# Two feature halves of a tile as one attention task, written to two ring banks and the two auxiliary banks

## The chip, the cores and the metric

The kernel runs on one core of a Trainium2 chip. The metric is the time of one execution on the device in microseconds; the figure for a kernel is the median of several executions. All arithmetic is in fp32.

In the profile, PE is TensorE (matrix products), PEld its loading of weights, ACT ScalarE, DVE VectorE, POOL GpSimd and SP the engine that starts most transfers. A "pass" is one matmul record of the profile: an fp32 matmul of the program with 256 columns is two passes, an fp32 transposition one.

## The reference

A graph attention block on x (128 graphs, 64 nodes, 512 features), with a 64 x 64 adjacency shared by all. The input is normalised first, the two attention layers follow, then a feed-forward part, a second normalisation and the residual:

```
h = relu(layernorm(x))
# layer 1, four heads
Wh = einsum('bnf,hfo->bhno', h, W_heads)            # 512 x 512 for each head
e  = leaky_relu(f1[..., :, None] + f2[..., None, :])  # f1, f2: Wh times the halves of a_heads
attn = softmax(where(adj > 0, e, -1e9))             # 64 x 64 for each graph and head
h = elu(einsum('bhnm,bhmo->bhno', attn, Wh))        # heads laid side by side: 2048 features
# layer 2: the same with W_out (2048 x 512) and one head
out = elu(gat(h, adj, W_out, a_out))
y = relu(out @ w1 + b1) @ w2 + b2 + out
result = x + layernorm(y) * gamma + beta
```

## The kernel before

128 rows of x, which are two graphs, are one tile; there are 64 tiles, and four of them are a group, so there are 16 groups. Two things matter for what follows.

First, layer 1 applies attention to the normalised input before it multiplies by the weights, since attn (h W) = (attn h) W. This "first attention" of a tile is a product of `HN[t]` (128 rows: two graphs of 64 nodes; 512 features) with the attention weights `AT[t]`. Each graph has only its own 64 rows, so a matmul here uses 64 of the 128 rows of TensorE's array, and the two graphs of a tile stand on rows 0 to 63 and 64 to 127. Their results go to two banks of PSUM.

Second, the large products (the four heads `g_a`, the second layer `g_b`, the feed-forward `g_c` and `g_d`) each multiply 2 x 2 blocks by a scheme of seven block products with sums before and after. The attention results `z` are therefore kept as blocks: "11" and "12" for the two feature halves of the first two tiles of a group, "22" for the second half of the last two, and "S1" for the sum of both halves of those (made beforehand in `HNS`).

PSUM is divided into a ring of six banks and two auxiliary banks:

```python
ps = ctx.enter_context(tc.tile_pool(name="ps", bufs=6, space=bass.MemoryType.PSUM))

def bank(name):
    return ps.tile([P, 2, T], FP, tag="mm", name=name)

def aux(shape, name):
    return ps.tile(shape, FP, tag="aux", name=name, bufs=2)
```

The ring holds the sums of the large products and the results of the first attention. The auxiliary banks take transpositions and small products. The transposition of the second layer's output, one for each tile of the group before, is one of them:

```python
def transpose_out(j):
    ...
    pt = aux([P, KC, P], f"pto{g}_{j}")
    for k in range(KC):
        nc.tensor.transpose(pt[:, k, :], o[:, j, ts(k, P)], ident)
    nc.scalar.copy(OT[j // 2][:, :, ts(j % 2, P)], pt)
    nc.gpsimd.tensor_tensor(o[:, j], o[:, j], b2s, ALU.add)
    if j == G - 1:
        bl[1] = blocks(OT, f"o{g}")       # sums of OT, on VectorE
```

The first attention has a task for each tile and feature half, eight in a group. A task takes two ring banks, makes four matmuls (two column blocks `c` for each of two graphs `b`), and ScalarE empties the first bank and VectorE the second:

```python
def task(j, half):
    t = G * g + j
    nm = ("11", "12")[half] if j < 2 else ("S1", "22")[half]
    ...
    src, off = (HNS[t], 0) if nm == "S1" else (HN[t], half * T)
    at = AT[t]
    banks = [bank(f"pz{nm}_{t}_{b}") for b in range(NB)]
    for c in range(2):
        for b in range(NB):
            rows = slice(b * N, (b + 1) * N)
            nc.tensor.matmul(
                banks[b][:, c, :].rearrange("p (h n) -> p h n", h=H),
                src[rows, off + c * P:off + (c + 1) * P],
                at[rows, b], start=True, stop=True, skip_group_check=True,
            )
    for b in range(NB):
        ...
        if b == 0:
            nc.scalar.copy(dst, srcv)
        else:
            nc.vector.tensor_copy(dst, srcv)
```

The statistics of the next tile's x and its normalisation run between these tasks: VectorE makes the statistics (`n1st`) of an x that a transfer must have brought, ScalarE writes `hn`, and this frees the buffer for the next x.

The main loop goes through the groups. While the products of layer 2 of group g run step by step (`project2(g)`, 28 steps of four matmuls each, named `g_b`), side work is laid between the steps: the first attention of group g + 1, the transpositions, feed-forward and output of group g - 1, and the scores of group g + 2:

```python
attn = attend1(g + 1) if g + 1 < NG else []
norms, scores, turns = stage_a(g + 2)
tr, ff, fin = feed_forward(g - 1) if g >= 1 else ([], [], [])
...
first = mix(attn, tr)
if g >= 1:
    first[5:5] = norms[:1]
    first[10:10] = norms[1:]
...
run(project2(g), first + mix(ff[:7] + early + ..., scores + [nothing] * 8) + ...)
```

`mix` merges lists evenly, and `run` spreads the side list evenly over the steps. The first group's attention has no loop to stand in and comes before it. A scheduler then sets each engine's order from priorities and dependences, so the order of the calls is not exactly that of the engine.

Of the kernel before, what the change touches and what calls it, by code (L numbers as in the profile page):

```python
# [9 lines left out]
FP = mybir.dt.float32  # L10
# [12 lines left out]
def gat_preln_kernel(  # L23
# [28 lines left out]
    nc = tc.nc  # L52
    P = 128
    B, N, F = x.shape
    H = W_heads.shape[0]
# [3 lines left out]
    NB = P // N  # L59
    KC = F // P  # L60
    NT = B * N // P
    G = 4
    NG = NT // G
    Q = O // 2
    T = 2 * P
# [6 lines left out]
    big = ctx.enter_context(tc.tile_pool(name="big", bufs=1))  # L72
# [5 lines left out]
# [5 lines that stand above are left out]
# [7 lines left out]
    X, HN, HNS, AT = {}, {}, {}, {}  # L90
# [156 lines left out]
    def flush_late():  # L247
        while late:
            late.pop(0)()

    def run(steps, side=()):

        side, done = list(side), 0
        for i, fn in enumerate(steps):
            fn()
            while done * len(steps) < (i + 1) * len(side):
                side[done]()
                done += 1
# [204 lines left out]
    def transpose_weights(p):  # L463
        A = A1.pop(p)
        for j in range(2):
            t = 2 * p + j


            pt = aux([P, NB * H, N], f"s1pt{t}")
            for h in range(H):  # L470
                to = pt[:, h:h + H + 2:H + 1] if h + 1 < H else pt[:, h:h + 2]
                nc.tensor.transpose(to, A[:, j, h:h + 2].rearrange("p b m -> p (b m)"), ident)  # L472
            AT[t] = big.tile([P, NB, H, N], FP, tag="at", name=f"at{t}", bufs=G)
            nc.scalar.copy(AT[t].rearrange("p b h n -> p (b h) n"), pt)  # L474
# [5 lines left out]
    def stage_a(g):  # L480


        if g >= NG:
            return [], [], []
        p, r = 2 * g, 2 * g + 1

        def norms(p):
            norm1(2 * p)
            norm1(2 * p + 1)
            if p >= 2:  # L490
                prefetch(2 * p + 2)
                prefetch(2 * p + 3)

        def transposes(p):
            transpose_h(2 * p)
            transpose_h(2 * p + 1)

        return (
            [lambda: norms(p), lambda: norms(r)],
            [  # L500
                lambda: transposes(p), lambda: transposes(r), nothing, lambda: project_f(g), nothing,
                lambda: (scores1(g), attn_weights(p)), nothing, lambda: attn_weights(r),
            ],
            [nothing, lambda: transpose_weights(p), nothing, nothing, lambda: transpose_weights(r)],
        )
# [4 lines left out]
    def attend1(g):  # L510
        z = {}
        ZB[g] = z

        def task(j, half):
            t = G * g + j
            nm = ("11", "12")[half] if j < 2 else ("S1", "22")[half]
            if nm not in z:
                z[nm] = big.tile([P, H, 2, T], FP, tag="z" + nm, name=f"z{nm}_{g}")
            src, off = (HNS[t], 0) if nm == "S1" else (HN[t], half * T)
            at = AT[t]  # L520
            banks = [bank(f"pz{nm}_{t}_{b}") for b in range(NB)]
            for c in range(2):
                for b in range(NB):
                    rows = slice(b * N, (b + 1) * N)
                    nc.tensor.matmul(  # L525
                        banks[b][:, c, :].rearrange("p (h n) -> p h n", h=H),
                        src[rows, off + c * P:off + (c + 1) * P],
                        at[rows, b], start=True, stop=True, skip_group_check=True,
                    )
            for b in range(NB):  # L530
                n0 = (j % 2) * P + b * N
                dst = z[nm][:, :, :, n0:n0 + N].rearrange("p h c n -> p c h n")
                srcv = banks[b].rearrange("p c (h n) -> p c h n", h=H)
                if b == 0:
                    nc.scalar.copy(dst, srcv)
                else:
                    nc.vector.tensor_copy(dst, srcv)

        return [lambda j=j, half=half: task(j, half) for j in range(G) for half in range(2)]


    H1, ZSUM = {}, {}
# [14 lines left out]
    def z_sums(g, h):  # L557
        z = ZB[g]
        ZSUM[h] = new_sums(f"z{g}_{h}")
        eng = nc.vector if (g, h) == (0, 0) else nc.gpsimd  # L560
        sums(eng, z["S1"][:, h], z["11"][:, h], z["12"][:, h], z["22"][:, h], *ZSUM[h])
# [71 lines left out]
    def scores2(g, j):  # L633
        if j == 0:
            F2[g] = sm.tile([P, 2, G], FP, tag="f2", name=f"f2_{g}")
        f = F2[g]
        for c in range(2):
            junk = wk.tile([P, FO], FP, tag="elu", name=f"jf{g}_{j}_{c}", bufs=3)
            nc.vector.scalar_tensor_tensor(  # L639
                junk, WH2[g][:, j], 1.0, ao[:, c, :], ALU.mult, ALU.mult,  # L640
                accum_out=f[:, c, j:j + 1],
            )

    def spread2(g):

        f = F2[g]
        dg = sm.tile([P, G, N], FP, tag="s2dg", name=f"s2dg{g}", bufs=1)
        nc.vector.tensor_tensor(
            dg, eye[:, None, :].to_broadcast([P, G, N]), f[:, 1][:, :, None].to_broadcast([P, G, N]),
            ALU.mult,  # L650
        )
        F2[g] = f, dg
# [26 lines left out]
    def stage_e(g):  # L679

        gap = [lambda: None]
        score = [lambda j=j: scores2(g, j) for j in range(G)]
        attend = [lambda j=j: attend2(g, j) for j in range(G)]
        return (
            gap + score + [lambda: spread2(g)] + gap * 2 + [lambda: softmax2(g)] + gap * 5
            + [lambda: transpose_weights2(g)] + gap * 2 + attend[0:2] + gap + attend[2:4] + gap * 3
        )
# [71 lines left out]
    def mix(*lists):  # L759

        lists = [l for l in lists if l]
        keyed = [((i + 0.5) / len(l), n, fn) for n, l in enumerate(lists) for i, fn in enumerate(l)]
        return [fn for _, _, fn in sorted(keyed, key=lambda k: k[:2])]
# [21 lines left out]
    softmax_end = LAST["A"]  # L785
    transpose_weights(0)
    attn = attend1(0)
    for fn in attn[:4]:
        fn()
    head0 = project1(0, 0)  # L790
    for fn in head0[:2]:
        fn()
    transpose_weights(1)
    for fn in attn[4:]:
        fn()
    z_sums(0, 0)

# [13 lines left out]
    def more_sums(m):  # L811
        fetch(m)
        weight_sums(m, softmax_end)
# [3 lines left out]
    for g in range(NG):  # L817
        if g >= 1:
            side = stage_e(g - 1)
        else:  # L820
            side = sum(stage_a(1), [])
            for i, m in ((5, 4), (9, 5), (12, 6), (17, 7)):
                side.insert(i, lambda m=m: more_sums(m))
        done, n = 0, 6 * H
        for i in range(n):
            if i % 6 == 0:
                steps = head0 if (g, i) == (0, 0) else project1(g, i // 6)
            if (g, i // 2) != (0, 0):
                steps[i % 6]()
            while done * n < (i + 1) * len(side):  # L830
                side[done]()
                done += 1
        flush_late()
# [3 lines that stand above are left out]
        if g == NG - 1:  # L837
            run(project2(g), tr + [nothing] * 6 + ff[:2])
            run(ff[2:], [
                lambda: [scores2(g, j) for j in range(G)], lambda: spread2(g), nothing, nothing,  # L840
                lambda: softmax2(g), *[nothing] * 7, lambda: transpose_weights2(g), nothing,
                *[lambda j=j: attend2(g, j) for j in range(G)], nothing,
            ])
            continue
        early = [lambda: z_sums(g + 1, 0)]
        first = mix(attn, tr)
        if g >= 1:
            first[5:5] = norms[:1]
            first[10:10] = norms[1:]
        if g == 0:  # L850
            def sums_late(m):
                fetch(m)
                weight_sums(m, LAST["A"])

            run(project2(g), first + early + norms + scores + turns + [
                load_rows, lambda: sums_late(M1), lambda: sums_late(M2)
            ])
        else:
            run(project2(g), first + mix(
                ff[:7] + early + ff[7:12] + fin[:1] + ff[12:13] + fin[1:2] + ff[13:],  # L860
                scores + [nothing] * 8,
            ) + mix(fin[2:], [nothing] + turns + [nothing] * 2))
    last = fin
    tr, ff, fin = feed_forward(NG - 1)
# [30 lines left out]
```

## Time and profile before

The kernel takes 2364.29 us, the median of three executions (2364.02 to 2364.8). The profiled execution has a span of 2360.4 us at a mean granted TensorE clock of 0.992.

| What | Value |
|---|---|
| first attention, pz and pzS (line 525), passes | 768 + 256 |
| ScalarE copy of one bank to z (line 535) | 585 ns, 96 for z and 32 for zS |
| VectorE copy of one bank to z (line 537) | 691 ns, 96 for z and 32 for zS |
| large products, one pass (lines 307, 322) | 379 to 385 ns recorded, 1.73 us from start to start for eight |
| transposition pto (line 700), records | 256, for 64 tiles |
| idle of the weight loads before line 525, put down to "issue" | 37.1 us in 119 places |

The times in a row of the profile are the lengths of single records. Records of TensorE overlap, since its passes are pipelined, so eight passes of 380 ns do not take 3 us. What eight passes cost is the distance from the start of the first to the start of what comes after them. "Issue" is idle time for which the profile shows no releaser: nobody was waited for.

### The profile page before, as it was taken

What the parts mean: (1) busy time and instruction counts of PE and PEld (TensorE: products, weight loads), DVE (VectorE), ACT (ScalarE), POOL (GpSimd) and SP (SyncE); (2) the same over time, 40 slices, a digit from 0 to 9 for tenths busy, and PEclk for the clock granted to TensorE, in tenths of its full rate; (3) what the DMA queues carried; (4) which work ended last, traced back from release to release, by engine and by line L of the source; (5) the groups of instructions that cost most, each with busy time, mean ns of one, the idle gap of its engine ahead of it and who ended that gap; (6) DMA issues with size and microseconds to landing.
All of it is one profiled execution on the core that took longest, in us unless ns stands there. A gap on an engine that the chain in (4) does not pass through costs nothing.

```text
span 2360.4 us, 32849 instructions
## 1 busy us (share of the span) xinstructions
PE 2317.9 (98%) x11805; PEld 1934.5 (82%) x11805; DVE 1265.5 (54%) x2210; ACT 911.0 (39%) x1623; POOL 1026.7 (43%) x917
## 2 busy tenths in 40 slices
PE   6989999999999999999999999999999999999997
PEld 4868787888878888787887878888788887878885
DVE  7625474554646556474554745556464563744527
ACT  2524425253352533425244251533525344251513
POOL 5664444416344353443524444253443534533333
PEclk7999999999999999999999999999999999999999
DMA  8545353444535445353444544435354453534443
GB/s 308 184 142 193 125 183 127 164 152 132 182 125 178 134 139 179 126 180 129 154 163 129 182 131 161 153 130 181 127 177 132 138 179 127 182 118 164 157 148 106
DMA packets 257809, 366.89 MB, mean 155 GB/s; under 512 B 22216, under 2 KB 145128, under 8 KB 257648
## 3 DMA queue, kind: packets, MB, share of 16 engines
q1 hardware_dynamic: 251024, 343.82, 43.9%
q0 software_dynamic: 4512, 16.78, 1.9%
q10 hardware_dynamic: 2112, 4.19, 0.5%
q8 instruction: 95, 1.56, 0.3%
q14 instruction: 66, 0.54, 0.1%
HBM read 337.45 MB, written 27.26 MB: 155 GB/s over the span
## 4 chain that ended last, share of the span: by engine, by line
PE 94%; DVE 2%; ACT 1%; POOL 1%; issue 0%; DMA 0%; DVEq 0%
PE g_b L322 33%; PE g_a L307 32%; PE g_c L307 8%; PE g_d L322 8%; PE pz L525 4%; PE pa L673 2%; PE pto L700 1%; PE pzS L525 1%; PE pth L371 1%; PE s1pt L472 1%; PE pf L381 1%; PE s1pe L406 1%; DMA x<-in_x_dram 0%; PE s2pt L667 0%; PE pwa L193 0%
## 5 line engine op out<-in xcount | busy, mean ns | idle before, releaser
L322 PE MATMUL g_b<-w,h 128*128 128x256 f32 x2560 | 598.1, 381 | 0.0
L322 PEld LDWEIGHTS g_b<-w,h 128*128 128x128 f32 x2560 | 480.5, 190 | 72.2 <-issue 10.1
L307 PE MATMUL g_a<-z,w 128*128 128x256 f32 x1520 | 361.0, 380 | 1.2 <-DVE g_a L581 0.7
L307 PE MATMUL g_a<-zs_z,w 128*128 128x256 f32 x1504 | 347.9, 379 | 0.0
L307 PEld LDWEIGHTS g_a<-z,w 128*128 128x128 f32 x1520 | 287.6, 190 | 57.9 <-issue 14.3
L307 PEld LDWEIGHTS g_a<-zs_z,w 128*128 128x128 f32 x1504 | 284.8, 190 | 50.5 <-issue 14.3
L322 PE MATMUL g_b<-w,hS 128*128 128x256 f32 x1024 | 243.5, 382 | 0.0
L585 POOL TENSOR_TENSOR hS<-hS,h 128x512 f32<-128x512 f32 x64 | 83.0, 1297 | 366.8 <-DVE hS L549 366.8
L547 ACT ACTIVATE exc<-g_a 128x512 f32<-128x512 f32 x256 | 152.3, 595 | 199.7 <-DVE g_a L581 119.6
L322 PEld LDWEIGHTS g_b<-w,hS 128*128 128x128 f32 x1024 | 191.4, 191 | 30.9 <-issue 6.7
L549 DVE SCALAR_TENSOR_TENSOR h<-exc,g_a 128x512 f32<-128x512 f32 x192 | 131.6, 686 | 136.3 <-ACT exc L548 136.2
L548 ACT ACTIVATE exc<-exc 128x512 f32<-128x512 f32 x256 | 161.6, 631 | 6.5
L615 POOL TENSOR_TENSOR h<-h,h 128x512 f32<-128x512 f32 x64 | 86.7, 1362 | 138.1 <-PE g_b L322 138.0
L332 POOL TENSOR_TENSOR zs_z<-zS,z 128x512 f32<-128x512 f32 x63 | 89.7, 1424 | 128.3 <-PE g_a L307 123.7
L615 POOL TENSOR_TENSOR h<-hS,h 128x512 f32<-128x512 f32 x64 | 81.1, 1268 | 142.4 <-PE g_b L322 142.4
L474 ACT COPY at<-s1pt 128x512 f32<-128x512 f32 x64 | 34.7, 588 | 279.8 <-PE s1pt L472 279.8
L307 PE MATMUL g_c<-ot,w 128*128 128x256 f32 x512 | 123.9, 385 | 0.8 <-DVE n2ve L347 0.8
L322 PE MATMUL g_d<-w,rt 128*128 128x256 f32 x512 | 121.5, 380 | 1.7 <-DVE o L740 1.0
L307 PE MATMUL g_a<-zS,w 128*128 128x256 f32 x496 | 117.2, 379 | 0.0
L639 DVE SCALAR_TENSOR_TENSOR jf<-wh,ao 128x512 f32<-128x512 f32 x128 | 94.3, 776 | 40.3 <-ACT wh L621 40.1
L333 POOL TENSOR_TENSOR zs_z<-z,zs_z 128x512 f32<-128x512 f32 x63 | 85.4, 1357 | 61.1 <-PE g_a L307 40.7
L307 PEld LDWEIGHTS g_c<-ot,w 128*128 128x128 f32 x512 | 93.9, 190 | 21.8 <-issue 9.3
(159 smaller groups left out, 3535.6 us busy)
## 6 DMA issues: line engine op xcount, KB each, us to landing
w<-tc SPq DMA_DIRECT2D x632, 256.0 KB, 2.6
w<-in_L_gnn_W_heads_dram SPq DMA_DIRECT2D x192, 256.0 KB, 2.7
w<-in_L_gnn_W_out_dram SPq DMA_DIRECT2D x192, 256.0 KB, 2.7
w<-in_L_gnn_w_dram SPq DMA_DIRECT2D x96, 256.0 KB, 2.7
x<-in_x_dram SPq DMA_DIRECT2D x66, 256.0 KB, 3.6
xr<-in_x_dram SPq DMA_DIRECT2D x64, 256.0 KB, 2.8
out_dram<-o SPq DMA_DIRECT2D x64, 256.0 KB, 2.1
tc<-pt POOLq DMA_DIRECT2D x20, 512.0 KB, 5.6
```

Of the source, the lines that this page charges most:

```text
L307: nc.tensor.matmul(bk[:, o, :], w[:, k, ts(o, P)], a[:, k, :], start=start and o == 0 and k == 0, stop=k == 1, skip_group_check=True,)
L322: nc.tensor.matmul(bk[:, j, :], a[:, k, ts(j, P)], w[:, k, :], start=start and k == 0 and j == 0, stop=i == len(ms) - 1 and k == 1, skip_g ...
L332: eng.tensor_tensor(s2, s1, a11, ALU.subtract)
L333: eng.tensor_tensor(s4, a12, s2, ALU.subtract)
L525: nc.tensor.matmul(banks[b][:, c, :].rearrange("p (h n) -> p h n", h=H), src[rows, off + c * P:off + (c + 1) * P], at[rows, b], start=True ...
L547: nc.scalar.activation(ex, src, AF.Relu, scale=-1.0)
L548: nc.scalar.activation(ex, ex, AF.Exp, scale=-1.0)
L549: nc.vector.scalar_tensor_tensor(dst, ex, -1.0, src, ALU.add, ALU.max)
L585: nc.gpsimd.tensor_tensor(dst, dst, H1["22"][:, h], ALU.add)
L615: nc.gpsimd.tensor_tensor(dst[:, h], x0[:, h], x1[:, h], ALU.subtract)
L639: nc.vector.scalar_tensor_tensor(junk, WH2[g][:, j], 1.0, ao[:, c, :], ALU.mult, ALU.mult, accum_out=f[:, c, j:j + 1],)
L673: nc.tensor.matmul(pa, AT2[g][:, j, :], WH2[g][:, j, :], start=True, stop=True)
```

## The change

The two tasks of a tile become one: eight matmuls on 64 rows follow each other, and then come the four copies. The first half is written to two ring banks as before, the second half to the two auxiliary banks, so that a task has four banks at once without taking four of the ring. It is meant to let TensorE do its work on 64 rows in longer runs. The side list has four tasks in place of eight; four empty entries keep its length, so that the other side work stands at the same steps as before. The attention of the first group is split in two blocks of two tiles, as before.

```diff
--- before.py
+++ after.py
@@ -511,32 +511,40 @@
         z = {}
         ZB[g] = z
 
-        def task(j, half):
+        def task(j):
+
             t = G * g + j
-            nm = ("11", "12")[half] if j < 2 else ("S1", "22")[half]
-            if nm not in z:
-                z[nm] = big.tile([P, H, 2, T], FP, tag="z" + nm, name=f"z{nm}_{g}")
-            src, off = (HNS[t], 0) if nm == "S1" else (HN[t], half * T)
             at = AT[t]
-            banks = [bank(f"pz{nm}_{t}_{b}") for b in range(NB)]
-            for c in range(2):
+            done = []
+            for half in range(2):
+                nm = ("11", "12")[half] if j < 2 else ("S1", "22")[half]
+                if nm not in z:
+                    z[nm] = big.tile([P, H, 2, T], FP, tag="z" + nm, name=f"z{nm}_{g}")
+                src, off = (HNS[t], 0) if nm == "S1" else (HN[t], half * T)
+                if half == 0:
+                    banks = [bank(f"pz{nm}_{t}_{b}") for b in range(NB)]
+                else:
+                    banks = [aux([P, 2, T], f"pz{nm}_{t}_{b}") for b in range(NB)]
+                for c in range(2):
+                    for b in range(NB):
+                        rows = slice(b * N, (b + 1) * N)
+                        nc.tensor.matmul(
+                            banks[b][:, c, :].rearrange("p (h n) -> p h n", h=H),
+                            src[rows, off + c * P:off + (c + 1) * P],
+                            at[rows, b], start=True, stop=True, skip_group_check=True,
+                        )
+                done.append((nm, banks))
+            for nm, banks in done:
                 for b in range(NB):
-                    rows = slice(b * N, (b + 1) * N)
-                    nc.tensor.matmul(
-                        banks[b][:, c, :].rearrange("p (h n) -> p h n", h=H),
-                        src[rows, off + c * P:off + (c + 1) * P],
-                        at[rows, b], start=True, stop=True, skip_group_check=True,
-                    )
-            for b in range(NB):
-                n0 = (j % 2) * P + b * N
-                dst = z[nm][:, :, :, n0:n0 + N].rearrange("p h c n -> p c h n")
-                srcv = banks[b].rearrange("p c (h n) -> p c h n", h=H)
-                if b == 0:
-                    nc.scalar.copy(dst, srcv)
-                else:
-                    nc.vector.tensor_copy(dst, srcv)
-
-        return [lambda j=j, half=half: task(j, half) for j in range(G) for half in range(2)]
+                    n0 = (j % 2) * P + b * N
+                    dst = z[nm][:, :, :, n0:n0 + N].rearrange("p h c n -> p c h n")
+                    srcv = banks[b].rearrange("p c (h n) -> p c h n", h=H)
+                    if b == 0:
+                        nc.scalar.copy(dst, srcv)
+                    else:
+                        nc.vector.tensor_copy(dst, srcv)
+
+        return [lambda j=j: task(j) for j in range(G)]
 
 
     H1, ZSUM = {}, {}
@@ -785,13 +793,13 @@
     softmax_end = LAST["A"]
     transpose_weights(0)
     attn = attend1(0)
-    for fn in attn[:4]:
+    for fn in attn[:2]:
         fn()
     head0 = project1(0, 0)
     for fn in head0[:2]:
         fn()
     transpose_weights(1)
-    for fn in attn[4:]:
+    for fn in attn[2:]:
         fn()
     z_sums(0, 0)
 
@@ -843,7 +851,7 @@
             ])
             continue
         early = [lambda: z_sums(g + 1, 0)]
-        first = mix(attn, tr)
+        first = mix(attn, tr, [nothing] * len(attn))
         if g >= 1:
             first[5:5] = norms[:1]
             first[10:10] = norms[1:]
```

## The prediction, made before the changed kernel ran

> **What bounds the kernel now.** I read the busy times first, then the chain of waits, then TensorE's waits, and last one stretch of TensorE's timeline instruction by instruction.
>
> ```profile
> PE 2317.9 (98%) x11805; PEld 1934.5 (82%) x11805; DVE 1265.5 (54%) x2210; ACT 911.0 (39%) x1623; POOL 1026.7 (43%) x917
> ...
> PE 94%; DVE 2%; ACT 1%; POOL 1%; issue 0%; DMA 0%; DVEq 0%
> ```
>
> TensorE is busy 98% of the span and makes up 94% of the chain; no other engine is above 54%. The list of TensorE's waits on others adds up to only some 34 us, and nearly all of it lies before 160 us or after 2300 us. Its longest entries:
>
> ```profile
> PE pzS L525 <- DVE z L537: 5.5, 1, 5.5
> PE s1pt L472 <- DVE s1A L435: 5.4, 1, 5.4
> PE pab L158 <- DMA ar<-in_L_gnn_a_heads_dram: 5.4, 1, 5.4
> ```
>
> So in the middle of the run time can only be won by giving TensorE less to do. The timeline of TensorE in the attention part of one group (start, length, what, number of passes) shows that it does more than its arithmetic there:
>
> ```profile
> 389.85 1.13 PE L525 MATMUL pz<-at,hn 64*128 64x256 f32 x8
> 390.91 1.99 PE L322 MATMUL g_b<-w,h 128*128 128x256 f32 x8
> 392.83 1.13 PE L525 MATMUL pz<-at,hn 64*128 64x256 f32 x8
> 393.90 0.66 PE L700 MATMUL pto<-ident,o 128*128 128x128 f32 x4
> 394.39 1.89 PE L322 MATMUL g_b<-w,h 128*128 128x256 f32 x8
> 396.21 1.13 PE L525 MATMUL pz<-at,hn 64*128 64x256 f32 x8
> 397.28 1.99 PE L322 MATMUL g_b<-w,h 128*128 128x256 f32 x8
> ```
>
> Read the starts. An undisturbed `g_b` step, between two others of full height, takes 1.73 from start to start (median of 167): eight passes of 0.216. A pz task is four matmuls on 64 rows. The two of a pair run on the two halves of the rows at once, so its eight passes are four pairs, which should take 4 x 0.216 = 0.864. It takes 1.06 or 1.07. The `g_b` step after it takes 1.92 where it stands between two pz tasks. One task and the step together: 1.07 + 1.92 = 2.99, where 0.864 + 1.73 = 2.59 would do. **0.40 us go to entering and leaving the 64-row form**, 0.20 each way. Cut finer, the starts in the task at 392.83 fall so: the last `g_b` pass starts at 392.52 and the first pz pair 0.31 later instead of 0.216; the second pair at 393.15 (0.32 later), the third at 393.37 and fourth at 393.58 (0.22, 0.21); the `pto` at 393.90 (0.32). At each change of form both the last interval before it and the first after it are 0.10 long. A short transposition takes 0.49 after a task against 0.44 elsewhere.
>
> **What the Trainium skill says.** "TensorEngine Tiling (Array Packing)", section Key Properties, says that a change of tiling mode, not of the tile, drains the TensorE. The trace agrees and gives the price, 0.20 per change. The same page under PSUM Bottleneck says that tiling makes TensorE faster but not the emptying of PSUM; here a 0.864 us task fills two banks that ScalarE and VectorE empty in 0.585 and 0.691 us, so it holds. "Perfetto Trace Analysis", section Tensor Engine Instruction (MATMUL, LD_WEIGHTS), says that TensorE's recorded ends are an estimate and that ScalarE and VectorE keep strict order. I therefore work with TensorE's starts; the order shows below, where a copy stands behind a waiting statistic.
>
> **The change part by part.**
>
> *Removed: changes of form.* Two tasks of four pairs become one of eight, so a group of four tiles has 4 entries and exits, not 8. Two tasks that already stand next to each other show that nothing is lost between them: in the first group pzS starts at 59.56 and the next pz at 60.52, 0.96 = 0.864 + 0.10, and only the entry's interval is in it. A long task then takes 1.07 + 0.864 = 1.93.
>
> In the built order of the changed kernel the sequence from the first task to the first `g_c` is: pz, g(1)+pto+g(3), pz, g(1)+pto+g(3), g, pz, g(1)+pto+g(3), g, pz, g(1)+pto+g(3), where g is a `g_b` step of four matmuls. That is 4 x 1.93 + 6 x 1.73 + 4 exits x 0.10 + 3 further entries x 0.10 + 4 pto x 0.44 = 7.72 + 10.38 + 0.70 + 1.76 = 20.56. Before, the same work from 388.19 to the `g_c` at 410.02 takes 21.83, and the exit of its last task puts another 0.10 on the `g_c`: 21.93. **Saved: 1.37 per group.** There are 15 loops with first attention; 14 of them look like this one (loop 0 has no pto and waits otherwise, see below). 14 x 1.37 = 19.2 us, all on the path, since TensorE is the path.
>
> *Added: a wait for an auxiliary bank.* The second half of a tile is now written to the two auxiliary banks, which are also those of pto, and pto comes right behind. In the built order each pto is put behind the first `g_b` matmul, and in all 56 cases waits for ScalarE: it takes the bank whose second-half copy ScalarE makes. Count from the task's start. The passes end by the record at 1.13 + 0.864 = 2.00. ScalarE's copy starts 0.04 after that (median over the present tasks) and takes 0.585: ends 2.63. TensorE starts about 0.06 after a release (136.28 to 136.34, and 54.53 to 54.58). So pto can start at 2.69. TensorE is there at 1.93 + 0.10 + 0.43 = 2.46, plus up to 0.10 if the exit costs both its intervals ahead of it; I use 2.55. Gap: 0.14 each, 56 x 0.14 = **7.8 us given back**. This is the term I trust least. The first half's copy is no trouble: it can start at 1.17 and is done at 1.75, before the second one is ready.
>
> *Moved: the order on ScalarE and VectorE.* ScalarE now does both copies, then `hn`, then `ot`. The `ot` of a tile is done some 4.0 after the task's start; the next task's second half, which needs that bank, starts 5.4 after it. VectorE's statistics of the next x wait for a DMA, as now:
>
> ```profile
> 394.00 0.58 ACT L535 COPY z<-pz 128x512 f32<-128x512 f32 x1 [1.63 <-PE pz L525]
> 395.02 0.70 DVE L343 BATCH_NORM_STATS2 n1st<-x 128x6 f32<-128x512 f32 x1 [3.21 <-DMA x<-in_x_dram]
> 395.64 0.68 DVE L537 COPY z<-pz 128x512 f32<-128x512 f32 x1
> ```
>
> Here a copy of z stood ready at about 394.0 and was made at 395.64, because the statistics stood ahead of it for 3.21 us. In the changed order both copies of the second tile stand behind it. By the same durations they are done about 8.8 after the first task's start; the first that needs their bank is the third tile, which starts at 10.7. About 2 us of room. The sums of `ot` on VectorE (1.6 to 1.8 us each beside GpSimd) have 2 to 3 us of room before the second `g_c` product.
>
> *Start.* In the first group the tasks already stand in two blocks, so no change of form is removed, but the later halves must wait for two auxiliary banks instead of the ring: one copy of 0.69 in each block, about +1 us together.
>
> *Loop 0.* TensorE waits 5.5 us at the third tile for VectorE, which stands in the statistics until x arrives at 135.0. In the changed order two copies rather than one stand between that arrival and the bank: 136.28 becomes some 137.5, but TensorE is then half a task further (1.06). I count 0.
>
> Sum: 2364.3 - 19.2 + 7.8 + 1.0 = **2353.9 us**.
>
> **The rivals.**
>
> *A: the wait for the bank takes all of it.* It needs 0.34 at each pto (19.2 / 56) instead of 0.14. For: the release comes within a fraction of a microsecond of the moment it is wanted, and anything on ScalarE ahead of the copy counts in full. Against: ScalarE is busy 39% and has nothing between the two copies. It would make about 2362 to 2364, and above if hn came first.
>
> *B: the wait is hidden and the full gain appears.* For: the exit's intervals may fall ahead of pto as a whole and the release may be a little earlier. Then 2345 to 2347.
>
> *C: VectorE becomes the bound in this stage*, because its copies bunch behind the statistics' DMA and the third tile waits for its auxiliary bank. If that happened in each group by 1 us, 14 us: about 2368. Against: the 2 us of room above, and VectorE's 54%.
>
> *D: the changes of form are hidden anyway.* Against it stands the regularity of the starts, 1.06 and 1.92 in each group, with no wait on anything. I give it little.
>
> **Range and chances.** The centre is the sum. B is the lower end, A the upper: 2345 to 2362. All rivals lie within 1% of the time before. 2% is 47 us, which is nearly all that the changes of form of 128 tasks cost (128 x 0.40 = 51), and the change takes away less than half of them. So within 2% is nearly sure.
>
> **What would show it.** Right: pz in blocks of 16 passes with 1.93 from start to start; the `pto` after a quarter of a `g_b` step; a new line among TensorE's waits, pto on ScalarE's z, of about 8 us over 56 times; the weight loads' idle time at the pz line (531 in the changed kernel) for "issue" about half its present 37 us. Wrong, if that new line is above 15 us or absent (A or B), if pz waits for VectorE in every group (C), or if blocks of 16 passes take 2.1 or more, which would be a cost between the halves that I left out.

## The result, and the profile after

The changed kernel takes **2359.15 us** (median of four executions, 2357.45 to 2361.88). The kernel before, run beside it, takes 2364.23 us (2364.02 to 2364.8). The ratio is 0.9979, with a 95% interval of 0.9962 to 0.9997: 5.1 us less, where 10.4 had been forecast. The sign was right and the size was half.

The share of busy time and the engines' share of the chain, from the profile of the changed kernel:

```profile
PE 2312.2 (98%) x11805; PEld 1938.7 (82%) x11805; DVE 1241.0 (53%) x2210; ACT 911.9 (39%) x1623; POOL 1022.9 (43%) x917
...
PE 92%; POOL 2%; DVE 2%; DMA 1%; ACT 1%; issue 1%; SPq 0%; DVEq 0%; POOLq 0%; ACTq 0%
```

TensorE still shows 98%. That number cannot tell what happened, as will be seen. The Trainium skill, "Perfetto Trace Analysis", section Identifying the Most-Contended Engine, says that the busy share of matmuls is no good measure of how close TensorE is to its limit, because matmuls are pipelined. The runs here agree: 98% is what the profiles of e4 (2340 us) and e5 (2332 us) show as well.

What TensorE waited for on other engines is spread over two lists, that of the matmuls and that of the weight loads ahead of them (what waited, for whom, total in us, times, longest). These are the lines of the matmuls that name a tile of the first attention or a `pto`, in the changed kernel:

```profile
PE pz L531 <- DVE z L545: 6.6, 2, 6.2
...
PE pto L708 <- ACT ot L709: 0.7, 1, 0.7
```

The second list, that of the weight loads, first before and then after:

```profile
PEld pz L525 <- issue: 27.0, 88, 0.3
...
PEld pto L700 <- issue: 18.5, 56, 0.3
...
PEld pzS L525 <- issue: 10.1, 31, 0.3
```

```profile
PEld pto L708 <- ACT z L543: 26.2, 56, 0.5
...
PEld pzS L531 <- issue: 10.1, 31, 0.3
PEld pz L531 <- issue: 9.9, 30, 0.3
```

Two things are to be seen. The gaps at the entries into the 64-row form were 27.0 + 10.1 = 37.1 us in 119 places and are 20.0 in 61: half, because there are half as many entries. And the 56 gaps of `pto` that had no releaser now have one, ScalarE's copy of `z`. The same wait is not in the matmuls' list at all.

The timeline of TensorE in the attention of one group (start, length, what, passes) shows what it costs:

```profile
388.57 2.00 PE L531 MATMUL pz<-at,hn 64*128 64x256 f32 x16
390.50 0.70 PE L322 MATMUL g_b<-w,h 128*128 128x256 f32 x2
391.29 0.66 PE L708 MATMUL pto<-ident,o 128*128 128x128 f32 x4
391.78 1.46 PE L322 MATMUL g_b<-w,h 128*128 128x256 f32 x6
393.17 2.00 PE L531 MATMUL pz<-at,hn 64*128 64x256 f32 x16
```

A block of 16 passes takes 1.93 from start to start. Then come two `g_b` passes, which should take 2 x 0.216 + 0.10 for the exit = 0.53. The `pto` starts 0.79 after them, so it is 0.26 late. In the four places of this group the distance is 0.79, 0.74, 0.80 and 0.74: on average 0.235 late. All 56 places are like this: the `pto` starts 2.72 after its task in 28 of them and 2.67 in the other 28. The `pto` itself takes 0.49 rather than 0.44. Together that is **0.28 to 0.29 at each `pto`**.

The releaser is in the timeline of all engines over the same stretch:

```profile
390.65 0.58 ACT L543 COPY z<-pz 128x512 f32<-128x512 f32 x1 [0.28 <-PE pz L531]
390.71 0.69 DVE L545 COPY z<-pz 128x512 f32<-128x512 f32 x1 [0.17 <-PE pz L531]
391.13 0.82 ACT L359 ACTIVATE hn<-x,n1nb,n1rs 128x512 f32<-128x512 f32 x1
391.29 0.42 PEld L708 LDWEIGHTS pto<-ident,o 128*128 128x128 f32 x4 [0.50 <-ACT z L543]
```

ScalarE's copy of the second half ends at 390.65 + 0.58 = 391.23, and the `pto` starts 0.06 later in the bank that this copy emptied.

By stage, from the starts in the two traces:

| Stretch | before | after |
|---|---|---|
| first pz from the start of the span | 49.05 | 50.21 |
| from there to the third group's pz (the first two groups' attention, with loop 0) | 196.18 | 195.66 |
| one group period, 13 times, each within 0.01 | 142.96 | 142.70 |
| of it, first task to the first `g_c` | 21.83 | 21.68 |
| from the last group's pz to the end | 256.7 | 256.4 |
| span | 2360.4 | 2357.4 |

The period is the measure to trust: it repeats thirteen times to a hundredth. The first pz, which no edit of this study touches, stands anywhere from 49.05 to 50.91 in the eleven traces.

### The profile page after: what moved, and what is told of

Same layout as the page of the kernel before. It is cut to its first block, busy times and chain, and to the rows that moved or that the text cites. A ratio compares the mean times of both kernels' runs of the same rounds, so it can differ in the third digit from the quotient of the medians.

```text
span 2357.4 us, 32812 instructions
## 1 busy us (share of the span) xinstructions
PE 2312.2 (98%) x11805; PEld 1938.7 (82%) x11805; DVE 1241.0 (53%) x2210; ACT 911.9 (39%) x1623; POOL 1022.9 (43%) x917
## 4 chain that ended last, share of the span: by engine, by line
PE 92%; POOL 2%; DVE 2%; DMA 1%; ACT 1%; issue 1%; SPq 0%; DVEq 0%; POOLq 0%; ACTq 0%
PE g_b L322 32%; PE g_a L307 31%; PE g_c L307 8%; PE g_d L322 8%; PE pz L531 4%; PE pa L681 2%; PE pto L708 2%; PE pzS L531 1%; PE s1pt L472 1%; PE pth L371 1%; ACT z L543 1%; PE s1pe L406 1%; DMA pw<-in_L_gnn_W_out_dram 1%; PE pf L381 1%; PE s2pt L675 0%
## 5 line engine op out<-in xcount | busy, mean ns | idle before, releaser
L322 PEld LDWEIGHTS g_b<-w,h 128*128 128x128 f32 x2560 | 479.1, 190 | 71.5 <-issue 10.1
L557 DVE SCALAR_TENSOR_TENSOR hS<-exc,g_a 128x512 f32<-128x512 f32 x64 | 44.0, 687 | 126.5 <-ACT exc L556 125.1
```

The source lines that it names most:

```text
L322: nc.tensor.matmul(bk[:, j, :], a[:, k, ts(j, P)], w[:, k, :], start=start and k == 0 and j == 0, stop=i == len(ms) - 1 and k == 1, skip_g ...
L557: nc.vector.scalar_tensor_tensor(dst, ex, -1.0, src, ALU.add, ALU.max)
```

## The theories

**W, the wait.** The longer blocks save what they should, and sharing the auxiliary banks with `pto` gives nearly all of it back. Then every way of freeing `pto` from that bank makes the kernel some 17 us faster than the changed one.

**B, the block.** Sixteen passes in a row, or the new order of the copies, cost something that the forecast left out. Then freeing `pto` gains little.

**R, the ring.** The auxiliary banks were needed: with all four banks out of the ring of six, the attention and the large products would wait for ring banks instead.

| Run | time, us | ratio to before (95%) | group period |
|---|---|---|---|
| before | 2364.23 | 1 | 142.96 |
| the change | 2359.15 | 0.9979 (0.9962 to 0.9997) | 142.70 |
| e1, `pto` a whole step later | 2342.59 | 0.9904 (0.9889 to 0.9919) | 141.55 |
| e2, `pto` in the ring | 2339.96 | 0.9891 (0.9877 to 0.9906) | 141.37 |
| e3, first half in the auxiliary banks | 2339.59 | 0.9893 (0.9876 to 0.9909) | 141.37 |
| e4, all four banks from the ring | 2340.09 | 0.9892 (0.9877 to 0.9907) | 141.37 |
| e5, two tiles in a block, ring | 2332.41 | 0.9864 (0.9849 to 0.9878) | 140.91 |
| e6, four tiles in a block, ring | 2355.54 | 0.9960 (0.9945 to 0.9975) | 142.5 |
| e7, VectorE frees the bank | 2373.86 | 1.0039 (1.0025 to 1.0053) | 143.91 |
| e8, e4 with the changes of form put back | 2365.45 | 1.0005 (0.9997 to 1.0014) | 143.20 |
| e9, e5 with a quarter in the auxiliary banks | 2335.18 | 0.9871 (0.9855 to 0.9888) | 141.17 |

e1 to e4 take the wait away in four ways, e7 lengthens it, e8 puts back the cost that the change removes, and e5, e6 and e9 ask how far the idea carries. Each ratio is against runs of the kernel before beside it.

## e1: `pto` behind a whole step

The change is left as it is, except for the place of `tr` (the `pto`) in the side list:

```diff
         if g >= 1:
-            first[5:5] = norms[:1]
-            first[10:10] = norms[1:]
+            n0, n1 = norms or [nothing] * 2
+            first = [
+                attn[0], nothing, nothing, tr[0], attn[1], n0, nothing,
+                tr[1], attn[2], nothing, n1, tr[2], attn[3], tr[3],
+            ]
```

> The changed kernel with each pto moved behind a whole g_b step (just ahead of the next task) instead of behind its first matmul; banks unchanged. Theory W (the wait of pto for the auxiliary bank that ScalarE empties costs 0.26 at each of 56 places and another 0.05 for starting again behind it): the wait is gone, a group takes 142.70 - 1.2 = 141.5 us, and the time falls by 14 x 1.2 = 17 us to about 2342. Rival B (the blocks of 16 passes or the changes of form themselves cost what is missing, the wait only stands where they would show anyway): a group stays at 142.7 and the time at 2358 to 2360. Rival O (later transpositions delay the feed-forward's sums): a new wait of g_c for VectorE, and less than half of the 17 us.

Measured: 2342.59 us (2341.66 to 2344.69), a period of 141.55. From the first task to `g_c` it is 20.52. The forecast had 20.56 for this stretch without any wait, so its sum of passes, entries and exits was right. TensorE's timeline shows the same block of 1.93, and no gap at `pto`:

```profile
386.40 2.00 PE L531 MATMUL pz<-at,hn 64*128 64x256 f32 x16
388.33 1.99 PE L322 MATMUL g_b<-w,h 128*128 128x256 f32 x8
390.16 0.60 PE L708 MATMUL pto<-ident,o 128*128 128x128 f32 x4
390.69 2.00 PE L531 MATMUL pz<-at,hn 64*128 64x256 f32 x16
```

The `pto` comes 1.83 after the step's start, which is 8 x 0.216 + 0.10 for the exit; it takes 0.44, and the 0.53 to the next task hold 0.10 for the entry besides. What the changed kernel takes beyond this, 21.68 - 20.52 = 1.16 per group, is the wait with the 0.05 of the slower start behind it. B is refuted here: blocks, copies and the auxiliary banks are those of the changed kernel. The expectation's rival O does not show either: the matmuls' list has 1.4 and 0.8 us of `g_c` waiting for VectorE in the whole run, against 1.3 and 0.8 in the changed kernel.

## e2: `pto` in a ring bank

```diff
-        pt = aux([P, KC, P], f"pto{g}_{j}")
+        pt = bank(f"pto{g}_{j}").rearrange("p a b -> p (a b)").rearrange("p (k q) -> p k q", k=KC)
```

> The changed kernel with pto written to a ring bank instead of an auxiliary one; the scheduler then sets it directly behind the task. Theory W: no wait for the task's own copies, pto costs 0.49 with the exit in it: a group 4 x 1.93 + 4 x 0.49 + 6 x 1.73 + 3 x 0.10 = 20.36 in this stretch instead of 21.67, so 141.4 us per group and about 2341. Rival B: 142.7 per group and 2358 to 2360. Rival R (six ring banks are too few when pto takes one too): a wait of pz or g_b for a copy of 0.3 or more in each group, and a time between the two.

Measured: 2339.96 us (2337.7 to 2341.73), period 141.37. The second halves stay in the auxiliary banks, and only their neighbour has gone. That is 1.33 per group less than the changed kernel, and 0.18 less than e1, where `pto` stands behind a `g_b` step: in e2, as in e3 and e4, it stands directly behind the block (see e4).

## e3: the first half in the auxiliary banks

```diff
-                if half == 0:
+                if half == 1:
                     banks = [bank(f"pz{nm}_{t}_{b}") for b in range(NB)]
```

> The changed kernel with the banks of the halves exchanged: first half in the auxiliary banks, second in the ring. ScalarE's copy of the first half ends some 1.80 after the task's start and TensorE is free for pto at 1.93, so Theory W expects no wait (or under 0.05): a group 141.4 and a time of about 2341. The next task's first half now needs the bank that ot is copied from, at about 4.14 by ScalarE's order, and starts at about 4.15: if that is late it costs up to 0.1 once in a group, 1.4 us in all. Rival B: 142.7 and 2358 to 2360.

Measured: 2339.59 us (2339.07 to 2341.41), period 141.37. `pto` still takes its bank from the attention, but from the half whose copies were done 0.86 earlier. The weight loads' list of e3 still names the copies:

```profile
PEld pto L708 <- ACT zS L543: 9.3, 28, 0.3
PEld pto L708 <- ACT z L543: 9.3, 28, 0.3
```

Together 18.6 us, yet this costs nothing. In e4, where `pto` shares no bank with the attention, the same gap of 0.33 is there without a releaser:

```profile
PEld pto L705 <- issue: 18.5, 56, 0.3
```

It is the exit from the 64-row form. A releaser's name beside a gap thus doesn't make it a loss; only the distance of the starts does.

## e4: all four banks from the ring

The long blocks alone, without the second part of the change:

```diff
-                if half == 0:
-                    banks = [bank(f"pz{nm}_{t}_{b}") for b in range(NB)]
-                else:
-                    banks = [aux([P, 2, T], f"pz{nm}_{t}_{b}") for b in range(NB)]
+                banks = [bank(f"pz{nm}_{t}_{b}") for b in range(NB)]
```

> The changed kernel with all four banks of a task from the ring, none from the auxiliary ones (the merging alone, without the second part of the change). Theory W: pto never waits; the second half of a group's first task waits for VectorE to read the last bank of the head before (about 0.3 once per group), so about 141.7 per group and 2345. Rival R (the ring of six is too small for tasks of four, which is what the auxiliary banks were taken for): waits of pz or g_b for z copies of 1 us or more in a group, and a time at or above 2359.

Measured: 2340.09 us (2338.84 to 2340.89), period 141.37. R is refuted: no wait for a ring bank appears in the groups, not even the 0.3 per group that the expectation had allowed for. TensorE's timeline:

```profile
387.49 2.00 PE L528 MATMUL pz<-at,hn 64*128 64x256 f32 x16
389.42 0.66 PE L705 MATMUL pto<-ident,o 128*128 128x128 f32 x4
389.91 1.89 PE L322 MATMUL g_b<-w,h 128*128 128x256 f32 x8
391.73 2.00 PE L528 MATMUL pz<-at,hn 64*128 64x256 f32 x16
```

Here `pto` follows the block directly, at 1.93, and takes 0.49. A tile's round from task to task is 4.24; in the changed kernel it is 393.17 - 388.57 = 4.60.

From the first task to `g_c` e4 takes 20.34. The work before takes 21.93 with the exit counted (the prediction's figure), so four entries and four exits fewer save 21.93 - 20.34 = 1.59, nearly 4 x 0.40; the periods say the same, 142.96 - 141.37. **The price of a change of form that the prediction read from the trace is what e4 collects.** The auxiliary banks, meant to make the long block possible, cost 142.70 - 141.37 = 1.33 per group: 1.16 for the wait, and the rest because the order built around them puts `pto` behind a `g_b` matmul, as in e1, rather than directly behind the block.

## e5: two tiles in one block

e4, and the blocks twice as long, so that a group has two entries and exits, not four:

```diff
-        return [lambda j=j: task(j) for j in range(G)]
+        return [lambda j=j: (task(j), task(j + 1)) for j in range(0, G, 2)]
...
+            first = [
+                attn[0], tr[0], no, no, tr[1], n0, no,
+                attn[1], tr[2], no, n1, no, tr[3], no,
+            ]
```

> All banks from the ring (as the third alternative above), and the tasks of two tiles as one block of 32 passes, two blocks in a group; the transpositions follow in later steps. If a change into the 64-row form and back costs 0.40 us whatever stands around it, two fewer of them in a group save 0.80: 141.38 - 0.80 = 140.58 per group and 2340.1 - 11 = about 2329. It also needs the two copying engines to keep up with TensorE inside a block (ScalarE 0.585 and VectorE 0.691 for each 0.864 of passes, and ScalarE's normalisation of 0.82 falls between them). Rival: they do not, pz waits for z copies inside the block, and the gain is under half of it.

Measured: 2332.41 us (2330.15 to 2335.29), period 140.91. This is the fastest version, 1.36% below the kernel before (interval 1.22 to 1.51%). The gain over e4 is 0.46 per group where 0.80 was possible. TensorE's timeline:

```profile
391.97 1.13 PE L528 MATMUL pzS<-at,hns 64*128 64x256 f32 x8
392.94 1.03 PE L528 MATMUL pz<-at,hn 64*128 64x256 f32 x8
393.80 1.10 PE L528 MATMUL pzS<-at,hns 64*128 64x256 f32 x8
394.67 1.15 PE L528 MATMUL pz<-at,hn 64*128 64x256 f32 x8
395.75 0.66 PE L705 MATMUL pto<-ident,o 128*128 128x128 f32 x4
```

The block takes 395.75 - 391.97 = 3.78 instead of 0.20 + 4 x 0.864 = 3.66. The quarters start on time (2.70 = 0.10 + 3 x 0.864), but their recorded lengths grow from 1.03 to 1.10 and 1.15: in the third quarter the second of the two passes that should run at once falls 0.07 behind, in the fourth 0.12, and so the last quarter takes 1.08 instead of 0.96. That is 0.24 per group. The lists name no releaser for it; e9 asks for its cause. The remaining 0.10 is that a change of form which ends in a transposition costs less than one that ends in a `g_b` step, see e8.

## e6: four tiles in one block

```diff
+        both = lambda: [fn() for fn in attn]
...
+            first = [
+                both, tr[0], no, no, tr[1], n0, no,
+                no, tr[2], no, n1, no, tr[3], no,
+            ]
```

> As e5_two_tiles, but all four tiles of a group as one block of 64 passes. By the price of changes alone 1.20 below the ring version: 140.2 per group and about 2323. Against it: VectorE's statistics stand between the copies and wait for an x that is only sent for when ScalarE has normalised the tile, so by the durations of the profile a bank is freed some 7.7 us after the block's start and wanted at 5.3; I expect 2 to 3 us of waiting of pz for VectorE in each group, and 2355 to 2370. If the first figure is measured, the copies are no limit.

Measured: 2355.54 us (2353.7 to 2356.55), periods from 140.77 to 144.34, mostly near 142.5. The matmuls' list of waits and TensorE's timeline:

```profile
PE pzS L528 <- DVE z L542: 28.9, 13, 11.4
```

```profile
397.07 1.14 PE L528 MATMUL pzS<-at,hns 64*128 64x256 f32 x8 [1.41 <-DVE z L542]
398.04 1.04 PE L528 MATMUL pz<-at,hn 64*128 64x256 f32 x8
399.01 0.66 PE L705 MATMUL pto<-ident,o 128*128 128x128 f32 x4
```

This block began at 389.76 and takes 9.25, where 0.20 + 8 x 0.864 = 7.11 would do: 2.1 are lost, as the expectation had it. By themselves the copies would keep up, since they empty two banks in about 0.7 and TensorE fills two in 0.864. But ScalarE has a normalisation for each tile besides (2 x 0.585 + 0.82 = 1.99, against 1.73 of TensorE), and VectorE has the statistics of the next x ahead of one of its copies and waits with them for the transfer, as its timeline shows:

```profile
395.73 0.69 DVE L343 BATCH_NORM_STATS2 n1st<-x 128x6 f32<-128x512 f32 x1 [2.26 <-DMA x<-in_x_dram]
396.35 0.67 DVE L542 COPY z<-pz 128x512 f32<-128x512 f32 x1
```

The copy ends at 397.02, and TensorE goes on at 397.07. In the blocks of the last two groups VectorE has no statistics to make, and they take 7.56 (still with ScalarE's normalisations) and 7.23 (without), where the twelve blocks before them take 9.07 to 10.47. So most of the loss is this wait, and not the length of the block. In the short blocks the same order of VectorE has room to wait; a block of sixteen banks has none. Of the 28.9 us, 11.4 fall in loop 0, where x comes late, and 17.5 in twelve later groups.

## e7: VectorE frees the bank

The copies change places: VectorE takes the bank that ScalarE had, and the other way round.

```diff
-                    if b == 0:
+                    if b == 1:
                         nc.scalar.copy(dst, srcv)
```

> The changed kernel with the copies of the two banks exchanged between ScalarE and VectorE, so that pto waits for VectorE (0.691 a copy instead of 0.585, started 0.06 later, and held up behind the statistics in the second tile). TensorE's work is the same. Theory W: pto 0.17 later in each of four places and some 0.5 in the second: a group 143.4 to 143.8 and a time of 2368 to 2374, slower than before the change. Rival B (the wait is only apparent): 142.7 and 2359.

Measured: 2373.86 us (2373.41 to 2374.31), period 143.91 in most groups (two of thirteen have 144.3 and 143.2): **the wait is now longer, and the changed kernel becomes slower than the one before.** The releaser in both lists follows the edit, and with the longer wait it appears in the matmuls' list too, half of the times:

```profile
PE pto L708 <- DVE z L545: 15.4, 28, 1.3
```

```profile
PEld pto L708 <- DVE z L545: 41.9, 56, 1.7
```

TensorE's timeline has a short and a long one:

```profile
390.19 0.70 PE L322 MATMUL g_b<-w,h 128*128 128x256 f32 x2
391.11 0.66 PE L708 MATMUL pto<-ident,o 128*128 128x128 f32 x4 [0.22 <-DVE z L545]
...
394.92 0.70 PE L322 MATMUL g_b<-w,h 128*128 128x256 f32 x2
396.58 0.66 PE L708 MATMUL pto<-ident,o 128*128 128x128 f32 x4 [0.96 <-DVE z L545]
```

The first is 0.92 behind the `g_b`, 0.13 more than in the same place of the changed kernel (0.79); VectorE's copy is 0.11 longer than ScalarE's (0.69 and 0.58). The second is 1.66 behind, 0.92 more (0.74), since VectorE, unlike ScalarE, has the statistics of the next x between its two copies:

```profile
394.16 0.69 DVE L545 COPY z<-pz 128x512 f32<-128x512 f32 x1 [3.10 <-PE pz L531]
394.76 0.68 DVE L343 BATCH_NORM_STATS2 n1st<-x 128x6 f32<-128x512 f32 x1
...
395.84 0.68 DVE L545 COPY z<-pz 128x512 f32<-128x512 f32 x1
```

The expectation had 0.17 more in each place and some 0.5 in the second. By the starts the four places have 0.12, 0.92, 0.05 and 0.11 more, 1.20 together, and the period grew by 1.21.

## e8: the price of a change of form

e4, with one transposition of 128 rows that nobody reads between the two halves of a tile, so that the form changes back and forth as often as before:

```diff
             for half in range(2):
+                if half == 1 and g >= 2:
+                    nc.tensor.transpose(aux([P, KC, P], f"pgap{t}")[:, 0, :], ident, ident)
```

> All banks from the ring, and in 14 groups one 128-row transposition of 0.11 us, whose result nobody reads, between the two halves of each task: one more pair of changes of form for each of 56 tiles, with hardly any work. Price per pair 0.40: a group 141.38 + 4 x 0.51 = 143.4, and about 2340.1 + 14 x 2.04 = 2369. Rival (the loss at a change belongs to the large products next to the tasks, not to the change): 141.38 + 4 x 0.11 = 141.8 and 2346.

Measured: 2365.45 us (2363.8 to 2370.68), period 143.20, which is 1.83 more than e4, where the rival of the expectation had 0.44. The inserted transpositions wait for no other engine. TensorE's timeline:

```profile
388.63 1.13 PE L530 MATMUL pz<-at,hn 64*128 64x256 f32 x8
389.69 0.33 PE L525 MATMUL pgap<-ident 128*128 128x128 f32 x1
389.95 1.14 PE L530 MATMUL pz<-at,hn 64*128 64x256 f32 x8
```

Each insertion costs 1.83 / 4 = 0.46. The transposition itself is a quarter of a `pto`, 0.44 / 4 = 0.11, so leaving and entering costs 0.35 and not 0.40. The difference is where the exit goes: into a `g_b` step it costs 0.10 behind the first pass, into a transposition 0.05 (a `pto` directly behind a block takes 0.49 and not 0.44). This also closes e5: it removes two such exits per group, 2 x 0.35 = 0.70, less 0.24 in the blocks = 0.46. The Trainium skill, "TensorEngine Tiling (Array Packing)", section Key Properties, says that changing the tiling mode drains TensorE; e8 shows the price by itself, 0.35 us for going out and back at passes of 0.216.

## e9: e5 with eight banks

Asks whether the 0.12 per block in e5 is a wait for ring banks:

```diff
-                banks = [bank(f"pz{nm}_{t}_{b}") for b in range(NB)]
+                if half == 0 and j % 2 == 1:
+                    banks = [aux([P, 2, T], f"pz{nm}_{t}_{b}") for b in range(NB)]
+                else:
+                    banks = [bank(f"pz{nm}_{t}_{b}") for b in range(NB)]
```

> e5 (two tiles as one block of 32 passes, all banks from the ring) with one thing changed: the first half of the second tile of each block goes to the two auxiliary banks, so a block uses six ring banks and both auxiliary ones, eight in all. This asks what the 0.12 us is by which each block of 32 passes in e5 (3.78 from start to the next start) exceeds its 3.66. If these are waits inside the block for ring banks whose copies are not done, a block now takes 3.66 to 3.70, the weight loads show no wait of pz or pzS on VectorE or ScalarE in the groups from 2 on, and the group period falls from 140.91 to some 140.70, the time from 2332 to about 2329. The auxiliary banks should do no harm here: they are filled by the third quarter of the block, which ends about 2.8 after its start; ScalarE, which has two earlier copies to make, is done with its one of them at about 3.45, and the transposition that wants it is there at 3.66 plus the exit. If the 0.12 is a cost of the long block itself, the block stays at 3.78 and the period at 140.9. If VectorE or ScalarE run later than this and the transposition behind the block waits, its distance to the next g_b step rises above 0.49 and the period goes up instead, to 141 or more.

Measured: 2335.18 us (2333.65 to 2336.02), period 141.17, 0.26 **more** than e5. TensorE's timeline, and ScalarE's in the timeline of all engines:

```profile
397.45 1.03 PE L531 MATMUL pz<-at,hn 64*128 64x256 f32 x8
398.66 0.66 PE L708 MATMUL pto<-ident,o 128*128 128x128 f32 x4 [0.18 <-ACT zS L543]
```

```profile
397.32 0.81 ACT L359 ACTIVATE hn<-x,n1nb,n1rs 128x512 f32<-128x512 f32 x1
...
398.04 0.57 ACT L543 COPY zS<-pzS 128x512 f32<-128x512 f32 x1
```

The last quarter's recorded length is 1.03 again, not 1.15, and from the third group on the last two passes of every block start 0.01 apart, where in e5 they start 0.13 apart or more. With eight banks its passes no longer stall: the 0.12 in e5 was a wait for a ring bank. For which copy it waited, neither run shows. But `pto` now comes 1.21 after the start of the last quarter, instead of 0.96: it waits for an auxiliary bank whose copy stands on ScalarE behind `hn`, which the expectation had left out of its count. Per block that is 0.25 lost and 0.12 won, 0.13 net, and 0.26 per group of two. The loss is where the third alternative of the expectation put it, except that it lies ahead of `pto` and not between `pto` and the next step. It is the mechanism of the changed kernel a second time.

## Why the prediction was half right

**The saving: right.** 1.37 per group was forecast for the order with `pto` behind a `g_b` matmul; e1, where `pto` also follows `g_b` passes but does not wait, takes 20.52 where 20.56 was said. Blocks took 1.93 as said, with nothing lost between the halves, and the entries' "issue" gaps fell to half.

**The wait for the auxiliary bank: right in place, wrong in size.** This is the step that failed, the term "0.14 each, 56 x 0.14 = 7.8 us given back". The forecast had `pto` start 2.69 after its task; in the group shown it starts 2.72, 2.67, 2.73 and 2.66 after. It had the releaser (ScalarE's copy), the number of times (56) and the 0.06 from release to start. What was off is the moment when TensorE would otherwise be there. The text worked out 2.46, then used 2.55 in case the exit costs both its intervals ahead of `pto`. It does, but both were counted already: the 1.93 of the block is 8 x 0.216 with 0.10 from the entry and 0.10 from the exit's first interval, and the 0.10 beside the 0.43 is the second. The allowance counted one of them twice, and 2.46 was right; e1 has the step behind the block at 1.83, with 0.10 for the exit and no more. That makes the wait 0.235 rather than 0.14. And `pto` after a wait takes 0.05 longer, a term that was not in the sum. So 0.28 to 0.29 at each `pto`, or 16 us over 56, stands where 7.8 was written.

The period confirms it. 1.37 saved less 4 x 0.28 is 0.25, and 142.96 - 142.70 = 0.26; the forecast had 1.37 - 0.56 = 0.81. Over fourteen groups that is 3.6 us instead of 11.4. The cautious choice of 2.55 was not cautious at all: it made the kernel look faster. A difference of 0.14 between two sums of 2.5 should have carried an error of its own of 0.1.

**Start and loop 0: too small to judge.** From the start of the span to the third group's pz it takes 245.23 before and 245.87 after, 0.64 more where 1.0 was forecast. But the first pz alone, which comes ahead of anything that the change touches, stands at 49.05 to 50.9 in the runs of this study, so this is no test. At the third tile of loop 0 TensorE waits 6.2 instead of 5.5 for VectorE, as the line above shows.

**The rivals** (by the letters of the prediction, which are not those of the theories above). A was nearest: it wanted 0.34 at each `pto` for everything to be lost, and 0.28 came. B needed a hidden wait and is what e1 measures, with 2342.6 below its 2345 to 2347. C does not show: all of pz's waits for VectorE lie ahead of 246 us, in the first group and loop 0. D is refuted by e4 and e8.

**What would show it.** The forecast said that a new line among TensorE's waits would tell, about 8 us if right and above 15 if wrong. The line is among the weight loads only, with 26.2 us (by the forecast's sign, A), and neither list gives the loss. A recorded matmul is 0.38 long and the next may start 0.216 after it, so the first 0.16 of a delay leave no gap between the records. In the changed kernel a delay of 0.26 leaves 0.09 (391.29 - 390.50 - 0.70), less than any entry of that list has (the shortest is 0.3); in e7 a delay of 1.66 - 0.53 = 1.13 is listed as 0.96. The weight loads' gap, 26.2 / 56 = 0.47, overstates: the starts give 0.28.

The total of 5.1 us for the medians stands beside 3.0 in the two profiled spans. The four executions of the changed kernel spread over 4.4 us, those of the kernel before beside them over 0.8, though the periods repeat to 0.01. Which part of the early stretch varies was not tried and stays open. To that extent it is luck that the medians make the gain half of the forecast: by the groups, which are what was reckoned, it is a third (3.6 of 11.4).

## What to carry to other kernels

When a change borrows a buffer from a pool, look first at who takes the next buffer from that pool, and when. Here the loan was not even needed (e4), and it ate 1.33 of the 1.59 us won in each group, as the borrowed bank was the last one to be emptied and the next to be wanted; borrowing it for the half that is emptied first (e3) cost nothing. Gaps on TensorE that repeat once per task are read from the distance between starts, not from the busy share or one list of waits: the Trainium skill, "Perfetto Trace Analysis", section Optimization Strategy, says that the same gap repeating on the engine that should be full can mean too few buffers. The 56 equal gaps at `pto` were not that: e3 removes them with the same banks in another order.

## What the runs showed of the hardware

- Going into the 64-row form and out of it costs 0.40 us when a 128-row product of 256 columns follows, and 0.35 when a 128-row transposition of 128 columns follows (e4, e8).
- A wait of TensorE shows at the weight load (0.50 in the line of the changed kernel, for a delay of 0.26) and may leave no trace at the matmul behind it. After it, four transpositions take 0.49 instead of 0.44, as they do behind an exit.
- Longer runs in the 64-row form pay only while the copies have slack. With six ring banks, 16 passes cost 1.93 as computed (e4), 32 cost 0.12 more than computed (e5), and 64 cost 2.1 more (9.25 and 7.11) where VectorE's statistics hold up a copy, but 0.45 and 0.12 more in the last two groups, which have none (e6).
